# A two-layer kernel on one core: other buffers for sorted tokens, another reciprocal root in the layer norm, and a second sequence that ends in two halves

## The chip, the core and the metric

The kernel runs on one core of a Trainium2 chip. The core has five engines that run side by side and wait for each other through semaphores: TensorE (PE in the profile) for matrix products, VectorE (DVE), ScalarE (ACT), GpSimd (POOL), and SyncE (SP), which here only issues transfers. The metric is the device time of one execution in microseconds (us); lower is better.

## The reference

Two transformer layers work on x of shape 2 x 1024 x 128 (two sequences of 1024 tokens), all in float32.

```python
x  = L0_attn_x
xn = layernorm(x)                                   # no gain, no bias
x  = x + attn0(xn) + ffn0(xn)
xn = layernorm(x)
x  = x + attn1(xn) + ffn1(xn)
```

- attn0: 16 heads of 8; queries, keys and values are xn times signs; a causal mask; the weight is sigmoid(4 * score / sqrt(8)), without a softmax.
- ffn0: softmax gate over 32 experts, 4 chosen per token, each an MLP 128 -> 64 -> 128 (silu(x w1 + b1) * (x w3 + b3), then w2), and a shared expert of width 128.
- attn1: projections, 16 heads, a relative position term with radius 128, softmax over all 1024 keys, output projection.
- ffn1: sigmoid gate over 16 experts, 4 chosen, each of width 176, and a shared expert of width 352.

## The kernel before

TensorE's order is written out by hand; the other engines' instructions are placed by a scheduler that follows their dependences. Within each engine instructions run in order, so an instruction that waits holds up all that stand behind it.

Layer 0's attention is a list of 96 steps (`steps0`: sequence, group of 4 heads, half of the queries, tile of 128 keys), the *cycles*. In cycle c TensorE computes scores (`scores0(c)`, L724), ScalarE takes the sigmoid (L730), GpSimd masks the diagonal tiles (L736), and one cycle later TensorE multiplies with the values (`values0(c-1)`, L751). A first half of queries has 4 cycles and a second half 8, of which the last 4 are on the diagonal and narrower. Cycles 48 to 95 are the second sequence's. All else in layer 0 is hung on this list: `at(c, f, ..., slot)` puts f before the scores of cycle c (slot 0), between scores and values (`MID`), or after the values (`END`).

Sequence 0's experts are computed densely: 34 *units*, each a pair of experts or the shared expert for 512 tokens. `open_unit` makes both first products (L359, L360) in one `big` tile of PSUM, then the activation, the product, and the weighting; `close_unit` (L387) makes the second product two cycles later in the `ffn` bank.

Sequence 1's tokens are sorted by expert. `scatter0` writes each normalized token to a slot in DRAM (GpSimd, indirect), and sixteen *quads* of four blocks of 128 slots are then computed, one every 1.5 cycles from cycle `QUADS`: `fetch0` (SP loads tokens and four weight blocks, cycle c-3), `turn0` (TensorE transposes the tokens, L639, and VectorE copies them out, L641; cycle c-1), `hidden0` (L651, with L657, L659 and L660 as activation), `outputs0` (L668; the next quad's cycle). From DONE + 2, `gather0` (L680) fetches each token's rows again and `gathered0` (L689) adds them, two per cycle. What a loaded weight set is good for ends with its outputs, so `fetch0` reuses the space of w1, w3 and w2 in turn.

PSUM has eight banks: three `big` tiles of two banks each, one `acc` bank for values, and one `ffn` bank that closing units, turns and hidden products share. `small()` is half of a `big` tile.

After the attention of sequence b, `added0` adds attention and shared expert (GpSimd), `merged0` transposes the sum into the residual x2s (L769, L770), `normed1` takes layer 1's norm, `turned1` transposes it (L253), and `blocks1` lists the six units of layer 1's shared expert. For the second sequence this follows cycle 96, together with the first ten `scan` steps of layer 1's attention (row maxima, L1173 on TensorE, L1193 and L1198 on VectorE), whose operands (`operands`, L1105) live in a pool that opens when layer 0's pool is closed. Then layer 1's main loop begins (first L1224), with 128 steps.

`layernorm` computes the reciprocal root with ScalarE's Sqrt (L235) and five short VectorE instructions (L237 to L241). Sqrt and Sigmoid are in different function tables, so ScalarE loads a table at each change. `turned_biases` (L514) transposes b1 and b3 and is the first thing that TensorE does; `biased0` (cycle 33) uses the result.

Of the kernel before, what the change touches and what calls it, by code (L numbers as in the profile page):

```python
# [10 lines left out]
F32 = mybir.dt.float32  # L11
AF = mybir.ActivationFunctionType
# [5 lines left out]
P = 128  # L18
# [30 lines left out]
def fused_layers_kernel(ctx: ExitStack, tc: tile.TileContext, a: dict, out: bass.AP):  # L49
# [39 lines left out]
    def quads(t):  # L89
        return t.rearrange("p (i c) -> p i c", c=P)  # L90
# [24 lines left out]
    w1 = load(l0, "w1", [P, E0 * I0])  # L115
    w3 = load(l0, "w3", [P, E0 * I0])
    b1 = load(l0, "b1", [P, M0])
    b3 = load(l0, "b3", [P, M0])
    w2 = load(l0, "w2", [P, M0, D], a["w2"].rearrange("(m p) d -> p m d", p=P))
# [103 lines left out]
    def layernorm(x, xn, pool, tiles=range(NT)):  # L223
# [6 lines left out]
        root = pool.tile([P, NT], F32, tag="ln_root", name="ln_root")  # L230
# [4 lines left out]
        nc.scalar.activation(root[:, c], var[:, c], AF.Sqrt)  # L235

        nc.vector.reciprocal(t[:, c], root[:, c])  # L237
        nc.vector.tensor_mul(t[:, c], t[:, c], var[:, c])
        nc.vector.tensor_add(t[:, c], t[:, c], root[:, c])
        nc.vector.tensor_scalar(t[:, c], t[:, c], 0.5, None, ALU.mult)  # L240
        nc.vector.reciprocal(rstd[:, c], t[:, c])  # L241
# [109 lines left out]
    def open_unit(weigh=nc.gpsimd):  # L351
# [12 lines left out]
        if ba is None:  # L364
            e = nc.scalar.activation(sg[0:m], hh[0:m, 0, :], AF.Sigmoid)
            last_exp["name"] = e.ins.name
            nc.scalar.copy(t[0:m], hh[0:m, 1, :])
            nc.vector.tensor_mul(sg[0:m], hh[0:m, 0, :], sg[0:m])
            nc.gpsimd.tensor_mul(h[0:m], t[0:m], sg[0:m])
# [138 lines left out]

    def turned_biases():
# [6 lines left out]
        return t  # L516
# [74 lines left out]
    def biased0(b):  # L591

        ps = small()
        for m in range(2):
            for h in range(2):
                for i in range(2):
                    nc.tensor.matmul(
                        ps[I0 * h:I0 * (h + 1), m * NBLK0 // 2:(m + 1) * NBLK0 // 2], b13[:, m, I0 * i:I0 * (i + 1)],
# [21 lines left out]
    def fetch0(g):  # L620
        w = l0.tile([P, 4, 2 * P], F32, tag=("w1", "w3", "w2")[g % 3], name="bw0")
# [4 lines left out]
        x = moe.tile([P, 4, P], F32, tag="t", name="bx0")  # L626
# [8 lines left out]
    def turn0(g):  # L635
        ps = quads(psum["ffn"].tile([P, TB], F32, tag="ffn", name="turn"))
# [6 lines left out]
    def hidden0(g):  # L643
# [9 lines left out]
        t = moe.tile([P, 4, P], F32, tag="h", name="bh0", bufs=4)  # L653
        sg, quad_h[g] = t[:, 0:2, :], t[:, 2:4, :]
# [36 lines left out]
    def blocks0(b):  # L691
        parts = [
            (P, w1[:, m * P:(m + 1) * P], w3[:, m * P:(m + 1) * P], w2[:, m, :], b1[:, m:m + 1],
# [66 lines left out]
    def added0(b):  # L760
        for q in range(NB):
            nc.gpsimd.tensor_add(yT0[b, q], yT0[b, q], attn0[b][:, q * TB:(q + 1) * TB])

    def merged0(b):
        x2s[b] = const.tile([P, NT, D], F32, tag=f"x2{b}", name=f"x2{b}")
        for q in range(NB):
# [10 lines left out]
    def turned1(b):  # L777
        xT1[b] = const.tile([P, T], F32, tag=f"xT1{b}", name=f"xT1{b}")
        transpose_tokens(xn1[b], xT1[b])
# [807 lines left out]
```

## Time and profile before

| | us |
|---|---|
| median of 3 runs (1307.63 to 1309.75) | 1308.75 |
| the profiled execution's own time | 1320.37 |
| its span, first to last instruction | 1318.5 |
| TensorE busy | 1171.2 (89%) |
| VectorE busy | 770.8 (58%) |
| ScalarE busy | 626.0 (47%) |
| GpSimd busy | 378.6 (29%) |
| mean granted TensorE clock | 0.945 |

An engine's busy time is the time covered by its instructions. In a list of waits, a line names the waiting instruction, what released it, the sum of the waits in us, their number and the longest. In a timeline, a line has the start and the time in us, engine, source line, operation, tile written and tile read, shapes and the number of instructions, and in brackets the idle time before and its releaser; "issue" means that no releaser was found. In a table of stages each engine has its busy time and its number of instructions; PEclk is the clock that TensorE was granted, as a share of full speed.

### The profile page before, as it was taken

To read this page: it belongs to the slowest core of one execution; us is meant where nothing else is said; L and a number is where in the kernel's file an instruction comes from. 1 tells how busy PE (TensorE), PEld (TensorE's weight loads), DVE (VectorE), ACT (ScalarE), POOL (GpSimd) and SP (SyncE) were. 2 spreads that over 40 slices of the span, in tenths; PEclk is the share of its full clock that TensorE was granted. 3 is DMA by queue.
4 is the path that set the end of the run, shared out by engine and by line. 5 is a ranking of instruction groups with operands and counts; after the bars stand their busy time and mean duration, and the time that the engine had idled before them with its cause. 6 is when DMAs were issued, how large, how long until landed. Compare 5 with 4: busy or idle time off the path is not lost.

```text
span 1318.5 us, 23960 instructions
## 1 busy us (share of the span) xinstructions
PE 1171.2 (89%) x8781; PEld 576.3 (44%) x8781; DVE 770.8 (58%) x2335; ACT 626.0 (47%) x1123; POOL 378.6 (29%) x482
## 2 busy tenths in 40 slices
PE   4889899887988778899799999998999999998997
PEld 1233233344432233434344444447999444443433
DVE  5564754446423377676876756754555766766563
ACT  2653344554555322464355644543444555554553
POOL 1124144410135342001002443330000345445463
PEclk9899999997998769899899998988999999998998
DMA  6955842334614250344265644658998255663510
GB/s 185 249 143 155 241 125 80 92 110 127 180 42 127 64 192 21 124 143 145 97 193 175 202 147 148 218 169 264 285 291 249 89 185 165 207 204 122 166 60 28
DMA packets 194472, 204.76 MB, mean 155 GB/s; under 512 B 26388, under 2 KB 176148, under 8 KB 194100
## 3 DMA queue, kind: packets, MB, share of 16 engines
q1 hardware_dynamic: 188052, 190.12, 46.9%
q0 software_dynamic: 6304, 13.12, 3.3%
q8 instruction: 69, 1.13, 0.4%
q14 instruction: 47, 0.39, 0.1%
HBM read 121.29 MB, written 90.42 MB: 161 GB/s over the span
## 4 chain that ended last, share of the span: by engine, by line
PE 67%; DVE 15%; DMA 5%; issue 5%; ACT 5%; POOL 2%; SPq 0%; DVEq 0%; POOLq 0%; ACTq 0%
PE sm L1234 11%; PE sm L1173 9%; PE acc L1253 8%; PE sm L1224 6%; PE big L724 5%; PE acc L751 4%; PE sm L975 4%; PE big L359 3%; DVE junk L1193 3%; PE big L360 3%; DVE maxima L1198 2%; PE ffn L387 2%; PE sm L1124 2%; DMA blockw<-wx 2%; PE sm L990 2%
## 5 line engine op out<-in xcount | busy, mean ns | idle before, releaser
L1241 ACT ACTIVATE p<-sm 128x512 f32<-128x512 f32 x512 | 264.7, 607 | 235.0 <-PE sm L1234 234.5
L1198 DVE TENSOR_REDUCE maxima<-sm 128x1 f32<-128x512 f32 (+3 forms) x472 | 226.8, 502 | 100.2 <-PE sm L1173 100.2
L730 ACT ACTIVATE at<-big 128x1024 f32<-128x1024 f32 (+1 forms) x192 | 145.1, 809 | 149.8 <-PE big L724 145.6
L1193 DVE CUSTOM_DVE_ANT_0 junk<-sm,near 128x384 f32<-128x384 f32 (+2 forms) x292 | 130.3, 446 | 69.7 <-PE sm L1173 69.7
L1253 PE MATMUL acc<-p,vs 128*32 128x512 f32 (+1 forms) x1288 | 147.2, 526 | 0.4 <-ACT yu L1265 0.4
L1224 PE MATMUL sm<-ident,near 128*128 128x128 f32 x704 | 109.3, 289 | 24.6 <-DVE maxima L1198 11.4
L1234 PE MATMUL sm<-qa,kls 32*128 32x512 f32 (+3 forms) x832 | 114.7, 569 | 0.0
L724 PE MATMUL big<-qm,xT 32*128 32x512 f32 (+3 forms) x768 | 108.1, 577 | 6.9 <-DVE h L373 4.0
L1173 PE MATMUL sm<-kls,qs 32*128 32x512 f32 (+2 forms) x776 | 108.0, 584 | 6.3 <-POOL kls L1105 5.3
L1224 PEld LDWEIGHTS sm<-ident,near 128*128 128x128 f32 x704 | 78.7, 144 | 79.2 <-ACT p L1241 35.4
L901 POOL DMA_INDIRECT got<-slots_y,slot_of x64 | 64.7, 1011 | 168.7 <-ACT p L1241 157.5
L751 PE MATMUL acc<-at,xn 128*32 128x512 f32 (+3 forms) x768 | 89.3, 540 | 21.4 <-POOL at L736 15.1
L736 POOL TENSOR_SCALAR_AFFINE_SELECT at<-at 128x512 f32<-128x512 f32 x64 | 41.9, 656 | 185.0 <-ACT at L730 184.6
L889 POOL DMA_INDIRECT slots_x<-xn,slot_of x64 | 62.4, 974 | 97.7 <-ACT p L1241 88.0
L1128 ACT COPY rel<-sm 128x512 f32<-128x512 f32 x112 | 57.5, 600 | 64.4 <-PE sm L1124 64.4
L911 POOL TENSOR_SCALAR got<-got,share 128x128 f32<-128x128 f32 x64 | 41.8, 654 | 109.3 <-DMA got<-slots_y,slot_of 109.0
L1173 PEld LDWEIGHTS sm<-kls,qs 32*128 32x128 f32 x776 | 37.1, 189 | 82.4 <-ACT p L1241 21.0
L1253 PEld LDWEIGHTS acc<-p,vs 128*32 128x32 f32 x1288 | 26.6, 109 | 106.2 <-issue 95.7
L1124 PE MATMUL sm<-posd,qs 32*128 32x256 f32 x448 | 57.4, 422 | 12.4 <-DVE maxima L1198 11.4
L724 PEld LDWEIGHTS big<-qm,xT 32*128 32x128 f32 x768 | 38.8, 198 | 67.0 <-issue 41.5
L1105 POOL TENSOR_SCALAR khs<-kf,not_aux,k_add 128x1024 f32<-128x1024 f32 x8 | 9.6, 1200 | 177.4 <-PE sm L1234 177.4
L1234 PE MATMUL sm<-qa,khs 32*128 32x512 f32 (+3 forms) x512 | 60.4, 507 | 0.0
(334 smaller groups left out, 1754.8 us busy)
## 6 DMA issues: line engine op xcount, KB each, us to landing
bounce<-rel SPq DMA_DIRECT2D x64, 768.0 KB
near<-bounce SPq DMA_DIRECT2D x64, 768.0 KB
blockw<-wx SPq DMA_DIRECT2D x53, 304.0 KB
slots_y<-by SPq DMA_DIRECT2D x35, 256.0 KB
cb<-cw SPq DMA_DIRECT2D x64, 128.0 KB
bw<-wx SPq DMA_DIRECT2D x64, 128.0 KB
room<-wx SPq DMA_DIRECT2D x26, 304.0 KB
slots_x<-zeros SPq DMA_DIRECT2D x19, 256.0 KB
```

What stands on the lines that cost most here:

```text
L724: nc.tensor.matmul(halves[r // 2][:, r % 2, off:TB], xT0[b][g, kt * P:(kt + 1) * P], masked[b, s][g, q * TB + off:(q + 1) * TB], start=Tru ...
L730: e = nc.scalar.activation(at[:, 2 * j:2 * j + 2, off:TB], sc[:, :, off:TB], AF.Sigmoid, scale=4.0 / math.sqrt(HD))
L751: nc.tensor.matmul(y[32 * r:32 * r + 32, off:TB], xn0[b][:, kt * P + 32 * r:kt * P + 32 * r + 32], at[:, r, off:TB], start=(kt == 0), stop ...
L901: d = nc.gpsimd.indirect_dma_start(y, None, slots_y[:, :], bass.IndirectOffsetOnAxis(ap=slot_of[:, t, j:j + 1], axis=0))
L1124: nc.tensor.matmul(ps[r][:, j, :], qs[g, t:t + P], posd[g, :], start=True, stop=True)
L1173: nc.tensor.matmul(ps[r][:, (k0 - lo) * P:(k1 - lo) * P], qs[g, qt * P:(qt + 1) * P], (kh if far else kl)[g, k0 * P:k1 * P], start=True, s ...
L1193: nc.vector.tensor_tensor_reduce(junk[:, 0:(k1 - k0) * P], part, near[n, i][:, r, w0:w0 + (k1 - k0) * P], 1.0, -BIG, ALU.add, ALU.max, mx[ ...
L1198: nc.vector.tensor_reduce(mx[:, r, slot:slot + 1], part, AX.X, ALU.max)
L1224: nc.tensor.matmul(ps[r][:, i * P:(i + 1) * P], near[n, i][:, r, w0:w0 + P], ident, is_transpose=True, start=(i == close[0]), stop=False, ...
L1234: nc.tensor.matmul(ps[r][:, i0 * P:i1 * P], k[g, kt * P:(kt + 1) * P], qa[n][g, i0 * P:i1 * P], start=(m == 0 and not close), stop=(m == l ...
L1241: e = nc.scalar.activation(p[:, r, :], ps[r], AF.Exp)
L1253: nc.tensor.matmul(y[rows_of(r), part], vs[:, kt, rows_of(r)], probs[n, kt][:, r, part], start=(kt == 0), stop=(kt == NT - 1 and part.stop ...
```

## The change

It has these parts, all but the norm within layer 0 and the passage to layer 1:

1. `turned_biases` moves from before cycle 0 to cycle 32, and `biased0` to 34.
2. w1, w3 and w2 are loaded in halves of their own. `fetch0` runs at c-5 and takes these six buffers in turn; tokens take four buffers. `turn0` transposes into a half of a `big` tile instead of the `ffn` bank. In `hidden0` the sigmoid and the product are two tiles. `QUADS` goes from 54 to 57.
3. The 34 units are spread over 38 cycles. `added0`, `merged0`, `normed1`, `turned1` and the gate of sequence 0 move by 3 to 6 cycles; projections of layer 1 move from two cycles after DONE to four before it.
4. Gathers start one cycle after DONE, their additions one cycle behind them. Eight units stand on the cycles after DONE (before, five, with three more at the end); their last product is on VectorE, without ScalarE's copy.
5. `added0`, `merged0`, `normed1`, `turned1` and `blocks1` of sequence 1 are split: the first 512 tokens at cycles 90 to 95, the rest after cycle 96.
6. The reciprocal root is made on VectorE: a first guess from the bits, and three Newton rounds.

```diff
-        root = pool.tile([P, NT], F32, tag="ln_root", name="ln_root")
-        nc.scalar.activation(root[:, c], var[:, c], AF.Sqrt)
-        nc.vector.reciprocal(t[:, c], root[:, c])
...
-        nc.vector.reciprocal(rstd[:, c], t[:, c])
+        bits = t.bitcast(I32)[:, c]
+        nc.vector.tensor_scalar(bits, var.bitcast(I32)[:, c], 1, None, ALU.arith_shift_right)
+        nc.vector.tensor_scalar(rstd.bitcast(I32)[:, c], bits, -1.0, float(0x5F3759DF), ALU.mult, ALU.add)
+        for _ in range(3):
+            nc.vector.tensor_mul(t[:, c], rstd[:, c], rstd[:, c])
+            nc.vector.tensor_mul(t[:, c], t[:, c], var[:, c])
+            nc.vector.tensor_scalar(t[:, c], t[:, c], -0.5, 1.5, ALU.mult, ALU.add)
+            nc.vector.tensor_mul(rstd[:, c], rstd[:, c], t[:, c])
...
-            nc.scalar.copy(t[0:m], hh[0:m, 1, :])
+            if weigh is nc.gpsimd:
+                nc.scalar.copy(t[0:m], hh[0:m, 1, :])
             nc.vector.tensor_mul(sg[0:m], hh[0:m, 0, :], sg[0:m])
-            nc.gpsimd.tensor_mul(h[0:m], t[0:m], sg[0:m])
+            weigh.tensor_mul(h[0:m], t[0:m] if weigh is nc.gpsimd else hh[0:m, 1, :], sg[0:m])
...
-        w = l0.tile([P, 4, 2 * P], F32, tag=("w1", "w3", "w2")[g % 3], name="bw0")
+        w = l0.tile([P, 4, 2 * P], F32, tag=("w10", "w11", "w30", "w31", "w20", "w21")[g % 6], name="bw0")
...
-        x = moe.tile([P, 4, P], F32, tag="t", name="bx0")
+        pool, tag = ((moe, "t"), (moe, "t"), (l0, "xn0"), (l0, "xT0"))[g % 4]
+        x = pool.tile([P, 4, P], F32, tag=tag, name="bx0")
...
-        ps = quads(psum["ffn"].tile([P, TB], F32, tag="ffn", name="turn"))
+        ps = quads(small())
...
-        t = moe.tile([P, 4, P], F32, tag="h", name="bh0", bufs=4)
-        sg, quad_h[g] = t[:, 0:2, :], t[:, 2:4, :]
+        sg, quad_h[g] = (moe.tile([P, 2, P], F32, tag="h", name=n, bufs=4) for n in ("bsg0", "bh0"))
...
-    b13 = turned_biases()
...
+    QUADS = 57
+    SPAN = QUADS - 6 - U0
     for i in range(HALF):
-        at(U0 + i, open_unit, nc.gpsimd if U0 + i < 30 else nc.vector, slot=MID)
-        at(U0 + 2 + i, close_unit, slot=END)
+        c = U0 + i * SPAN // HALF
+        at(c, open_unit, nc.gpsimd if c < 30 else nc.vector, slot=MID)
+        at(c + 2, close_unit, slot=END)
...
+    at(32, turned_biases, slot=MID)
+    at(34, biased0, 1, slot=MID)
...
-    QUADS = 54
-        at(c - 3, fetch0, g, slot=END)
+        at(c - 5, fetch0, g, slot=END)
...
-        at(DONE + 2 + i // 2, gather0, 1, i, slot=END)
-        at(DONE + 4 + i // 2, gathered0, 1, i, slot=END)
+        at(DONE + 1 + i // 2, gather0, 1, i, slot=END)
+        at(DONE + 2 + i // 2, gathered0, 1, i, slot=END)
...
-    at(DONE + 2, projections, 0, slot=MID)
-    at(DONE + 2, queries, 0, 0, slot=END)
+    for i in range(8):
+        c = DONE + 1 + 2 * i
+        at(c, open_unit, nc.vector, slot=MID)
+        at(c + 2, close_unit, slot=END)
+    at(DONE - 4, projections, 0, slot=MID)
+    at(DONE - 2, queries, 0, 0, slot=END)
...
-    for i in range(5):
-        at(DONE + 4 + 3 * i, open_unit, slot=MID)
-        at(DONE + 6 + 3 * i, close_unit, slot=END)
...
-    at(N_ATT + 1, added0, 1)
-    at(N_ATT + 2, merged0, 1)
+    at(90, added0, 1, (0,))
+    at(91, merged0, 1, (0,), slot=END)
+    at(92, normed1, 1, FIRST)
+    at(94, turned1, 1, (0,), slot=END)
+    at(95, blocks1, 1, (0,))
+    at(N_ATT + 1, added0, 1, (1,))
+    at(N_ATT + 2, merged0, 1, (1,))
+    at(N_ATT + 2, normed1, 1, LAST)
...
     at(N_ATT + 3, operands, 0, 0)
+    at(N_ATT + 3, cleared1)
...
-    at(N_ATT + 3, normed1, 1)
+    at(N_ATT + 4, turned1, 1, (1,), slot=MID)
+    at(N_ATT + 5, blocks1, 1, (1,))
...
-    at(SCAN + 2, turned1, 1, slot=MID)
-    at(SCAN + 3, blocks1, 1)
-    for i in range(6):
-        at(SCAN + 3 + i, open_unit, slot=MID)
-        at(SCAN + 5 + i, close_unit, slot=END)
+    for i in range(3):
+        at(SCAN + 1 + 2 * i, open_unit, nc.gpsimd, slot=MID)
+        at(SCAN + 3 + 2 * i, close_unit, slot=END)
```

## The prediction

> **What bounds the kernel now.** I read four views: busy time by stage, the list of TensorE's waits, the timeline around the longest waits, and the chain that ended last. From 524.6 us on, where layer 1's main loop begins, the change alters neither the work nor its order, so that stretch (793.9 us to the end of the 1318.5 us span) is taken as constant and all terms lie before it. The stages below are: cycles 48 to 53 of layer 0, the sixteen quads (cycles 54 to 77), the tail of layer 0 (78 to 95), and the passage to layer 1.
>
> ```profile
> core 0: us, PE busy (x) PEld busy (x) DVE busy (x) ACT busy (x) POOL busy (x), PEclk, DMA share, GB/s
> 238.95:260.82 21.87, 16.12 (x121) 6.63 (x120) 9.00 (x34) 12.52 (x16) 9.60 (x12) 0.95 0.22 67
> 260.82:372.92 112.10, 94.92 (x805) 49.44 (x804) 53.39 (x156) 59.28 (x102) 10.38 (x16) 0.92 0.46 131
> 372.92:460.24 87.32, 71.36 (x398) 24.76 (x394) 25.88 (x52) 41.03 (x64) 43.60 (x48) 0.84 0.26 80
> 460.24:524.62 64.38, 51.80 (x215) 22.57 (x211) 50.19 (x150) 16.33 (x29) 21.88 (x34) 0.84 0.28 98
> ```
>
> TensorE is the busiest engine in every stage, but idles 5.8 + 17.2 + 16.0 + 12.6 = 51.5 us, and its granted clock is below 1: (1 - clock) x busy gives 0.8 + 7.6 + 11.4 + 8.3 = 28 us. So about 80 us of these 286 us are waits and their aftermath; that is all the change can win here. In the last stage VectorE is nearly as busy, and becomes the floor. What TensorE waits for:
>
> ```profile
> PE big L514 <- DMA b<-in_b_dram: 16.2, 1, 16.2
> PE acc L751 <- POOL at L736: 15.1, 9, 4.4
> PE turn L639 <- issue: 11.4, 6, 3.6
> ...
> PE acc L751 <- ACT at L730: 6.4, 3, 2.9
> ...
> PE turn L639 <- PE big L668: 2.5, 3, 0.8
> ```
>
> No entry names the loads of tokens (bx) or of expert weights (bw). Three of these waits in the timeline:
>
> ```profile
> 16.24 0.37 PE L514 MATMUL big<-ident,b 128*16 128x128 f32 x1 [16.24 <-DMA b<-in_b_dram]
> ...
> 19.68 4.85 PE L724 MATMUL big<-qm,xT 32*128 32x512 f32 x16 [2.00 <-DVE qm L717]
> ```
> ```profile
> 267.82 0.35 DVE L660 SCALAR_TENSOR_TENSOR bh<-hidden,bias,bh 128x128 f32<-128x128 f32 x1
> 268.27 0.63 PE L639 MATMUL turn<-ident,bx 128*128 128x128 f32 x4 [3.60 <-issue]
> 268.83 1.90 PE L724 MATMUL big<-qm,xT 32*128 32x512 f32 x8
> ```
> ```profile
> 391.99 0.96 POOL L680 DMA_INDIRECT got<-slots_y,slot  x1 [0.30 <-issue]
> 392.96 0.64 POOL L736 TENSOR_SCALAR_AFFINE_SELECT at<-at 128x512 f32<-128x512 f32 x1
> ...
> 393.66 1.08 PE L751 MATMUL acc<-at,xn 128*32 128x256 f32 x8 [4.43 <-POOL at L736]
> ...
> 394.67 2.08 PE L387 MATMUL ffn<-h,sdw 128*128 128x512 f32 x2
> ```
>
> First: TensorE's first instruction transposes a bias that lands at 16.2 us, with the token transposes queued behind it. Second: the "issue" wait is the one ffn bank; the turn starts 0.1 us after L660, the bank's last reader, ends (268.17). Third: the causal mask stands behind gathers on POOL.
>
> **The change part by part** (minus is a gain).
>
> *Start.* turned_biases goes from before cycle 0 to cycle 32. The first four normalized tiles then set the start. bv_q's arrival (7.35 us) still stands in VectorE's order, now after two of the three rounds; 14 small instructions took 1.25 us there, so the 16 left take about 1.5 us (8.8), normalizing 4 tiles and the masks between them about 2 us (10.9), transposes to 11.4, the copy 0.7 and qm 0.5 with what stands between: first scores near 13.5 instead of 19.7. **-6** (ends -3, -6.6). The two transposes and copy reappear at cycle 32, under 1.2 us, beside attention work.
>
> *Loads.* w1, w3, w2 in halves: three more SP issues of 0.43 to 0.9 us early, moving later constants by 2 us; the first expert unit runs at 99.6 us. 0. Fetching at c-5 instead of c-3, six weight and four token buffers: SP's wait for an old quad's weights (41.3 us at L632) goes, but TensorE never waited for these loads. 0; if the cover went (quads faster than the four 128 KB loads), it would show as hidden waiting for bw.
>
> *Units of sequence 0* spread over 38 cycles instead of 34. From 160 to 240 us TensorE is busy 79 of 80 us; the work, about 7 us of it, moves to cycles 48 to 51 and is paid there. 0 (-2 to +2), as some of it fills the 3.0 us of mask waits there.
>
> *Quads.* turn0 takes a big bank, so TensorE does the next scores (1.1 us) before it needs the ffn bank for hidden0. sg and h as two tiles let the second sigmoid start without waiting for the first product (0.8 us, as at 267.03). Of the nine turn waits (13.9 us) I leave 1.7 us, from the longest: 3.6 - 1.1 - 0.8. Late next: hidden's copy bxT (3.0 us in two waits, kept; layer 1's gate still stands before it on VectorE), and a new coupling: scores, turn and outputs now rotate over three big banks, ten allocations per three cycles instead of eight. I allow 16 x 0.2 = 3 us. Idle 17.2 -> 9.
>
> *Layer norm without Sqrt.* Seven table loads of 1.28 us go from ScalarE's list. Where cycles are short (254 to 264 us, four of them) one wait of 2.7 us goes. VectorE gets 14 short instructions instead of 5 per call, each about 0.2 us with its dependence: +1.8 us per call, hidden in the quads (VectorE 53 of 112 us). Not hidden is the call for the last half-sequence: turned1 stands before the scans in TensorE's order, with only some 5.4 us of matmuls between merge and turn. Here a rule speaks against the change. The row: VectorE's ln_t steps at 469.6, 470.2 and 471.4 took 0.56, 1.20 and 0.98 us beside POOL's 1.2 us operand instructions, 0.16 us elsewhere. The Trainium skill, "SBUF — State Buffer", section "Who interferes with whom", says that a VectorE instruction with two SBUF inputs is blocked for the whole of a GpSimd instruction that reads SBUF. By the rule all nine products of the call could each lose a POOL instruction, +9 us; by the changed order POOL has only four long ones there (kls, khs, vs, h: 4.7 us) and the eight statistics, with one input, run beside them first. I take +3.
>
> *Tail.* It is shorter by three cycles and holds eight units instead of six opened. Their last product goes from POOL (1.27 us each) to VectorE (0.69), and ScalarE's copy (0.58) goes. POOL then has 32 gathers at 1.25 us pitch, 11 masks of 0.64, two additions of 1.27: 49.6 us, against about 54 us of TensorE work (scores and values 24, units 25, the rest 5, from their rows). gathered0 stands one cycle after its gather instead of two; landing takes 2.5 us, and VectorE already waits 50.1 us for gathers here. Behind those waits stand the two products that free a unit's big bank. Projections move ahead of DONE past the last quads, without new work; by_position's bounce writes stay behind the quads' fetches on SP. I leave 9 of 16.0 us idle.
>
> *Passage.* Half of the second sequence's merge, norm and transpose and two units (6 us of TensorE) move into layer 0. VectorE: 50.2 us now; minus half the norm 5.5, two sigmoid products 1.4, half a merge and a copy 1.4; plus the steps 2.6 and one product 0.7: 45.2 us, 33 of them the ten scans' maxima. The operands come before the 16 memsets (2.4 us on POOL). With VectorE as floor and the wait for the norm ahead of the scans, about 52 us instead of 64.4: **-12** (-3 to -17).
>
> *Clock.* The row: after the 4.43 us wait L387 took 2.08 us where it takes 1.12 elsewhere, and L360 follows at 1.02; after the 2.50 us wait at 408.4 it again took 2.08. The Trainium skill, "TensorE: Matmul & The Clock Gate", Part 1, says that the clock halves after an idle window of about 3.4 us. By the rule only the four or five longest waits cost extra, some 1.7 us each (half a window, an estimate from the page), 8 us in all; by the rows 28 us run slow. I take the rows: shorter waits also matter. Half of the slow time of cycles 48 to 95 (19.8 us) stays.
>
> *Sum for cycles 48 to 96.* TensorE's work at full clock: 182.4 - 19.8 = 162.6 us; plus 7 (moved from earlier, saved there) and 7 (two units, half a merge and half a transpose from the passage): 176.6. Plus idle 3 + 9 + 9 and slow 10 = 207.6, against 221.3: -13.7, with the 7 saved earlier -21. Counting the matmuls of each changed cycle by their full-clock rows instead gives 172.5 + 24 = 196.5, hence -32. I take the first, since its stages are measured: **-21** (-8 to -34).
>
> Total -6 - 21 - 12 = **-39 us** on the profiled execution (1320.4 us, span 1318.5). The median of the runs, 1308.75 us, is 0.9% below it; scaled, -38.7: about 1270 us.
>
> **The rivals.**
> *The waits move.* hidden0 waits where turn0 did, masks wait behind gathers as before, and only the start (-6), the tables (-3) and some of the passage (-6) come: 1294 us. For it: one ffn bank remains, POOL is 49.6 us full, VectorE waits for gathers. Against: 1.1 us of scores between. 19%.
> *Slower: scores wait for ScalarE in the bank rotation.* With a turn between, scores take a bank that the previous cycle's sigmoid has to have read. The second sigmoid ends 2.1 us after its scores end (275.68, 277.79); TensorE has about 3.2 us (hidden, values, outputs) in between. Beyond 1.1 us more delay each cycle pays; over 24 cycles the gain of 38 us is gone at 1.6 us a cycle. At the 2.7 us of the one wait for L730, it costs 65: 1308.75 + 27 = 1336 us. ScalarE is busy 59 of 112 us. 7%.
> *The change does more than its waits*: the count by matmuls holds and the passage reaches VectorE's floor: -6 - 32 - 17 = -55, 1254 us. 17%.
>
> **Numbers.** Forecast case 57%, 1270 us (1258 to 1284). Slower by over 0.2% (2.6 us, about what a measurement of this kernel can tell from no change): 8%, the bank case and 1% of the case where the waits move; within it: 2%, of the latter too; faster: 90%. The range reaches to both gaining rivals: 1252 to 1296.
>
> **What would show it.** First L724 near 13.5 us; no Sqrt table load; turn with no wait for bh's readers; quads at 4.2 instead of 4.7 us a cycle; attention's last values near 433 us; main loop from about 486 us. Wrong would be: big banks waiting for L730 every cycle, hidden waiting for bw, or a passage over 60 us.

## The result, and the profile after

The changed kernel takes 1292.43 us (median of 4 runs, 1290.72 to 1295.13); beside it the kernel before took 1308.19 us (4 runs). The ratio is 0.9887, 95% interval [0.9855, 0.992]. Measured again later, in a set of its own, it was 1289.47 us against 1309.98, ratio 0.9839 [0.9795, 0.9883]. So the change saves 16 to 21 us. The forecast was 39 us (1270 us); the measured time lies inside the range, near its slow end. The ratios leave out executions more than 1.5% above the fastest of their kernel as slow, which among all kernels here strikes only two of the six of e_sqrt (its ratio would be 0.983 with them).

The profiled execution took 1295.13 us (span 1293.0, mean clock 0.956). First its table of stages, with columns as before. The quads start three cycles later now, so the rows are cycles 48 to 56, the quads (57 to 80), the tail of layer 0 (81 to 95), and the passage to layer 1.

```profile
core 0: us, PE busy (x) PEld busy (x) DVE busy (x) ACT busy (x) POOL busy (x), PEclk, DMA share, GB/s
226.14:253.84 27.70, 26.18 (x171) 8.47 (x171) 8.57 (x12) 15.47 (x20) 8.71 (x10) 1.00 0.48 145
253.84:361.79 107.95, 100.34 (x828) 55.68 (x825) 59.86 (x205) 60.51 (x104) 10.64 (x16) 0.95 0.40 116
361.79:436.29 74.50, 62.99 (x360) 22.02 (x359) 33.72 (x84) 33.25 (x53) 36.78 (x43) 0.93 0.30 92
436.29:505.79 69.50, 47.03 (x192) 20.03 (x191) 49.56 (x147) 10.35 (x19) 19.73 (x33) 0.78 0.28 95
```

Layer 0 as a whole behaves as forecast: TensorE idles 1.5 + 7.6 + 11.5 = 20.6 us in the first three rows (39 before), the clock there is 0.93 to 1.00, and attention ends at 436.3 us instead of 460.3. The last row is the surprise. In the passage TensorE is *less* busy than before (47 us against 52), with six units in it instead of eight. And yet the passage is 5 us *longer*, with 22.5 us idle and a clock of 0.78.

The list of TensorE's waits in the quads has lost its nine turn waits (13.9 us); this is what stands there now (who waits, for whom: us in all, times, longest):

```profile
PE hidden L659 <- DVE bh L667: 3.9, 2, 3.6
PE hidden L659 <- DVE bxT L649: 2.2, 3, 1.6
```

And the list for the passage, whose first entry was not there before:

```profile
PE big L256 <- DVE xn L246: 8.7, 1, 8.7
PE big L1184 <- DVE maxima L1204: 2.9, 3, 1.4
PE big L1219 <- DVE negmax L1212: 2.2, 1, 2.2
PE big L777 <- POOL yT L769: 2.0, 1, 2.0
```

L256 is the transpose of the last half-sequence (`turned1`, L253 before). It stands ahead of the scans in TensorE's order and waits for the last normalized tile. The timeline just before shows what that tile was late for:

```profile
451.46 1.26 POOL L373 TENSOR_TENSOR h<-t,sg 96x512 f32<-96x512 f32 x1 [0.67 <-DVE ln_t L242]
451.49 1.28 DVE L243 TENSOR_SCALAR ln_t<-ln_t 128x4 f32<-128x4 f32 x1
452.71 1.20 POOL L1116 TENSOR_SCALAR kls<-kf,not_aux,k_add 128x1024 f32<-128x1024 f32 x1
452.80 0.19 DVE L244 TENSOR_TENSOR ln_rstd<-ln_rstd,ln_t 128x4 f32<-128x4 f32 x1
453.03 0.90 DVE L241 TENSOR_TENSOR ln_t<-ln_rstd 128x4 f32<-128x4 f32 x1
453.89 1.19 POOL L1116 TENSOR_SCALAR khs<-kf,not_aux,k_add 128x1024 f32<-128x1024 f32 x1
453.96 1.13 DVE L242 TENSOR_TENSOR ln_t<-ln_t,ln_var 128x4 f32<-128x4 f32 x1
455.03 1.03 POOL L1119 COPY vs<-vf 128x1024 f32<-128x1024 f32 x1
455.12 0.96 DVE L243 TENSOR_SCALAR ln_t<-ln_t 128x4 f32<-128x4 f32 x1
456.12 0.16 DVE L244 TENSOR_TENSOR ln_rstd<-ln_rstd,ln_t 128x4 f32<-128x4 f32 x1
...
456.32 1.11 DVE L246 TENSOR_SCALAR xn<-x,ln_mv,ln_rstd 128x128 f32<-128x128 f32 x4
...
456.81 1.15 PE L256 MATMUL big<-ident,xn 128*128 128x128 f32 x4 [8.68 <-DVE xn L246]
```

Read the two engines against each other. Each VectorE step has 4 elements per partition and needs 0.16 us when it is alone. Four of them take about 1 us here, and each begins within 0.35 us after a GpSimd instruction of 1.0 to 1.3 us has begun and ends just after it. I call such a step *held*. Not every step beside GpSimd is: L244 at 452.80 also begins just after kls and takes 0.19 us, and these rows don't show why. kls, khs and vs in these rows are the *second* set of operands, `operands(0, 1)`, which the program lists six cycles after the first; GpSimd's order has it right behind the memsets and a unit's product. From the merge of the half-sequence (442.13) to its last tile (457.43) the norm takes 15.3 us.

### The profile page after: what moved, and what is told of

The parts are those of the page before. It is cut to its first block, busy times and chain, and to the rows that moved or that the text cites. A ratio compares the mean times of both kernels' runs of the same rounds, so it can differ in the third digit from the quotient of the medians.

```text
span 1293.0 us, 24010 instructions
## 1 busy us (share of the span) xinstructions
PE 1161.0 (90%) x8781; PEld 577.1 (45%) x8781; DVE 782.9 (61%) x2420; ACT 613.0 (47%) x1102; POOL 370.4 (29%) x475
## 4 chain that ended last, share of the span: by engine, by line
PE 63%; DVE 19%; DMA 8%; issue 5%; ACT 3%; POOL 2%; SPq 0%; POOLq 0%; DVEq 0%; ACTq 0%
PE sm L1245 11%; PE sm L1184 8%; PE acc L1264 8%; PE sm L1235 5%; PE big L731 4%; PE acc L758 4%; PE sm L984 4%; DVE maxima L1209 3%; PE big L362 3%; DVE junk L1204 3%; PE sm L1135 3%; PE big L363 2%; DMA got<-slots_y,slot_of 2%; PE ffn L391 2%; DMA room<-wx 2%
## 5 line engine op out<-in xcount | busy, mean ns | idle before, releaser
L1204 DVE CUSTOM_DVE_ANT_0 junk<-sm,near 128x384 f32<-128x384 f32 (+2 forms) x292 | 130.3, 446 | 64.3 <-PE sm L1184 63.9
L1184 PE MATMUL sm<-kls,qs 32*128 32x512 f32 (+2 forms) x776 | 105.8, 572 | 6.7 <-POOL kls L1116 5.4
L1184 PEld LDWEIGHTS sm<-kls,qs 32*128 32x128 f32 x776 | 36.5, 186 | 80.8 <-ACT p L1252 21.1
L1135 PE MATMUL sm<-posd,qs 32*128 32x256 f32 x448 | 58.1, 422 | 11.9 <-DVE maxima L1209 10.9
L1245 PE MATMUL sm<-qa,khs 32*128 32x512 f32 (+3 forms) x512 | 60.9, 509 | 0.0
```

The costliest lines, as they stand in the source:

```text
L1135: nc.tensor.matmul(ps[r][:, j, :], qs[g, t:t + P], posd[g, :], start=True, stop=True)
L1184: nc.tensor.matmul(ps[r][:, (k0 - lo) * P:(k1 - lo) * P], qs[g, qt * P:(qt + 1) * P], (kh if far else kl)[g, k0 * P:k1 * P], start=True, s ...
L1204: nc.vector.tensor_tensor_reduce(junk[:, 0:(k1 - k0) * P], part, near[n, i][:, r, w0:w0 + (k1 - k0) * P], 1.0, -BIG, ALU.add, ALU.max, mx[ ...
L1245: nc.tensor.matmul(ps[r][:, i0 * P:i1 * P], k[g, kt * P:(kt + 1) * P], qa[n][g, i0 * P:i1 * P], start=(m == 0 and not close), stop=(m == l ...
```

## Experiments

Three questions were open: whether layer 0's parts are worth what the sum said; why the passage grew; and whether it is bounded by VectorE's work. Theory A: TensorE waits in the passage because the transpose stands ahead of the scans. Theory C: the norm is long because GpSimd's instructions hold its small steps. Rival B: VectorE's work is a floor, so that neither matters. The times in the table are from one profile of each kernel; "first scan" and "passage" count from attention's last values, and the passage ends where the main loop starts.

| kernel | ratio to before | attention ends | first scan | passage | main loop from |
|---|---|---|---|---|---|
| before | 1 | 460.3 | +13.1 | 64.3 | 524.6 |
| before, again (r_before) | 1 | 460.7 | +13.1 | 64.3 | 525.0 |
| changed | 0.9887 [0.9855, 0.992] | 436.3 | +25.0 | 69.5 | 505.8 |
| changed, again (r_after) | 0.9839 [0.9795, 0.9883] | 431.0 | +24.5 | 68.7 | 499.7 |
| bias transposes first (u_bias) | 0.9912 [0.9882, 0.9942] | 437.7 | +25.3 | 68.6 | 506.3 |
| turns in the ffn bank (u_bank) | 0.9901 [0.9864, 0.9939] | 438.6 | +26.1 | 71.8 | 510.4 |
| Sqrt on ScalarE (e_sqrt) | 0.9796 [0.9743, 0.985] | 436.3 | +21.2 | 64.7 | 501.0 |
| late turn (e_turn_late) | 0.9827 [0.9784, 0.987] | 438.9 | +18.0 | 64.5 | 503.4 |
| second operands after the norm (e_pool) | 0.9823 [0.9774, 0.9873] | 433.3 | +23.6 | 68.1 | 501.4 |
| quiet GpSimd (e_quiet) | 0.979 [0.9747, 0.9834] | 432.9 | +19.6 | 65.1 | 498.0 |
| quiet, late turn (e_quiet_late) | 0.977 [0.9726, 0.9814] | 438.9 | +14.8 | 60.3 | 499.2 |
| the same with Sqrt (e_quiet_late_sqrt) | 0.9813 [0.9779, 0.9848] | 432.7 | +15.2 | 61.8 | 494.5 |
| units behind the scans (e_units_after) | one run | 428.8 | +26.1 | 79.1 | 507.9 |
| part 5 undone (u_split) | 0.9749 [0.9707, 0.9791] | 427.3 | +7.8 | 60.9 | 488.2 |
| the same, second operands late (u_split_quiet) | 0.9726 [0.9678, 0.9774] | 429.6 | +7.7 | 60.9 | 490.5 |
| units' product on GpSimd (u_late_start) | 0.9892 [0.9838, 0.9946] | 434.3 | +26.2 | 70.9 | 505.3 |

Two yardsticks come first.

**The kernel before, again.**

> The kernel before once more, for a second profile. The first profiled execution took 1320 us, 11.6 us over its median; the changed kernel's two profiles were within 3 us of theirs. If the first profile of before was simply a slow execution, this one is nearer to 1310 us, and attention ends a few us before 460 and the main loop takes less than 794 us; the passage (64.3 us) should stay within 2 us, since its waits are of a fixed length. If the main loop takes 794 us again, then the change does alter it (782 to 789 us in all kernels with the change).

It took 1312.61 us (span 1310.9), with attention's end and the passage the same within 0.4 us. Its main loop took 1310.9 - 525.0 = 785.9 us instead of 793.9. So the 8 us by which the first profile was longer lay in the main loop alone, which the change doesn't touch (782 to 794 us in all these kernels).

**The changed kernel, again.**

> The changed kernel itself, for comparison with the three others on the same chip. It was 0.9887 of the kernel before; on the chip of the first experiments, where that kernel takes some 1312 us, this would be 1297 us. Its passage was 69.5 us; two variants with the same passage code (bias transposes first; turns in the ffn bank) had 68.6 and 71.8 us, with TensorE waiting 11.3 us for the norm instead of 8.7, so I expect 68.5 to 72 us here. No theory separates on this run.

The passage is the same (68.7 us, of which 8.2 us is the wait for xn), but attention ends at 431.0 instead of 436.3 us. The code is the same; the last three half-passes of attention, from about 345 us on, took 87.7 us here and 90.9 us there, and up to 92.8 us in the other kernels that share this code. A difference of less than 5 us in attention's end, seen in one profile each, therefore says nothing. In both profiles TensorE waits 8 to 9 us for xn. In u_bias, u_bank and u_late_start below, whose passage has the same code, it waits 11.3 us: there one more step, the shift L238, was held for 3.60 us, and merge to last tile takes 16.2 us instead of 14.9 to 15.3.

**Undo the start (part 1).**

```diff
-    at(32, turned_biases, slot=MID)
+    turned_biases()     # before cycle 0
```

> The changed kernel with the bias transposes back ahead of cycle 0, nothing else undone. If the start is worth what the two profiles show (first scores at 12.6 us instead of 19.7), the run is 6 to 7 us slower than the changed kernel (1298 to 1300 us) and the profile shows the first instruction waiting for b1 and b3 until about 16 us. If later waits absorb the start (cycles paced by loads or by the gate), it is less than 3 us slower.

The first scores come at 19.85 us instead of 12.61: the 7.2 us are there. But after the third half-pass of attention only 2.8 us were left, at cycle 48 4.3 us (6.0 against the second profile), and the ratio is higher than the changed kernel's by 0.0025 to 0.0073, 3 to 10 us, within intervals that overlap. The start's gain is real; how much of it reaches the end was not resolved.

**Undo the banks of the turn (part 2).**

```diff
-        ps = quads(small())
+        ps = quads(psum["ffn"].tile([P, TB], F32, tag="ffn", name="turn"))
```

> The changed kernel with turn0 back in the one ffn bank, all else as changed (loads ahead, two tiles for sigmoid and product). If the bank was the cause of the turn waits (13.9 us before), the quads get 6 to 12 us longer than the changed kernel's 108 us, and turns wait again for bh's readers. If the separate tiles had already removed the waits, or the bank rotation gives it back, it is within 2 us.

In this kernel's list of TensorE's waits the old entry is back:

```profile
PE turn L647 <- issue: 10.8, 6, 4.4
```

From the last values of cycle 51 to those of cycle 75 it takes 108.2 us instead of 102.3, so the banks are worth 5.9 us there. At attention's end 2.3 us are left, which is within the spread just named. In no kernel with the change do scores wait for the sigmoid each cycle: the forecast's slower rival did not occur.

**Undo the move of the units' product (part 4).** This is the kernel labelled u_late_start, a name that does not describe it.

```diff
-        at(c, open_unit, nc.vector, slot=MID)
+        at(c, open_unit, nc.gpsimd, slot=MID)
```

> The changed kernel, with the last product of the eight units on the last cycles of layer 0 back on GpSimd (and ScalarE's copy with it), as before the change. I counted GpSimd as 49.6 us full in that stretch and the move to VectorE as part of the gain there. If GpSimd's gathers set the pace of the tail, eight products of 1.27 us delay the gathers by up to 10 us, and attention ends 3 to 10 us later, with masks waiting behind gathers again; ratio higher than the changed kernel's by 0.002 to 0.007. If TensorE's own work and its clock set it, as the spread of the tail between executions of the same code suggests (87.7 to 92.4 us), attention ends within 3 us of the changed kernel's 431 to 439 us and the ratio is the same within its interval.

The last gather is issued at 437.0 us and attention ends at 434.3 us. Both lie between the two profiles of the changed kernel (433.3 and 438.8 us, 431.0 and 436.3 us), and the ratio lies in its interval. GpSimd doesn't pace the tail by more than the spread.

**The turn later (theory A).**

```diff
-    at(N_ATT + 4, turned1, 1, (1,), slot=MID)
-    at(N_ATT + 5, blocks1, 1, (1,))
+    at(N_ATT + 7, turned1, 1, (1,), slot=MID)
+    at(N_ATT + 8, blocks1, 1, (1,))
...
-        at(SCAN + 1 + 2 * i, open_unit, nc.gpsimd, slot=MID)
-        at(SCAN + 3 + 2 * i, close_unit, slot=END)
+        at(SCAN + 3 + 2 * i, open_unit, nc.gpsimd, slot=MID)
+        at(SCAN + 5 + 2 * i, close_unit, slot=END)
```

> The changed kernel with the second half's transpose (turned1 of sequence 1, blocks 1) three cycles later, behind the first scans, and its three units two cycles later. Theory A, the passage lost the gain because TensorE stands before that transpose waiting for the norm (8.7 us) while the scans queue behind it: the scans start some 5 to 8 us earlier and the run is 5 to 8 us faster than the changed kernel (about 1286 us). Theory B, VectorE is the floor of the passage in any order: the wait moves to the maxima and the time stays within 2 us of the changed kernel's.

The wait for xn is gone and the passage falls to 64.5 us. But the first scan still starts 18.0 us after attention, 5 us later than in the kernel before. In the list of waits of its passage a closing unit has taken the place:

```profile
PE ffn L391 <- POOL h L373: 3.3, 1, 3.3
```

That h is a product on GpSimd, which waits for a product of VectorE (L372) that stands between the norm's held steps. So A is true and not the whole.

**Sqrt back (part 6 alone undone).** `layernorm` as before the change, all else as changed.

> The changed kernel with the layer norm of before: Sqrt on ScalarE and five short VectorE steps instead of fourteen. If the fourteen steps on VectorE are what makes the last norm long, the passage gets 3 to 5 us shorter, and the tables cost 2 to 4 us among the quads: within 2 us of the changed kernel in all. If the tables are the larger part, it is 3 to 6 us slower.

The passage is 64.7 us, and merge to last tile takes 11.5 us: six short instructions, one of them on ScalarE, offer GpSimd less to hold than the fourteen of Newton's rounds. ScalarE has 23 table loads of 1.28 us in its order here against 10 with Newton, and yet layer 0 ends at 436.3 us, as in the first profile of the changed kernel. The ratio is lower by 0.004 to 0.009 (0.001 to 0.006 with all executions). So no gain from the tables that part 6 avoids is seen, though one of a few us would be lost in the spread of attention's end.

**GpSimd out of the way (theory C), in two steps.** First, the second set of operands waits for the last normalized tile (`last_norm`, recorded in `layernorm`):

```diff
-            nc.gpsimd.tensor_scalar(t, kf, ...)
+            e = nc.gpsimd.tensor_scalar(t, kf, ...)
+            if (b, s) == (0, 1):
+                tc.add_manual_dep(e.ins, last_norm["name"], ...)
...
-        nc.gpsimd.tensor_copy(vs, v)
+        e = nc.gpsimd.tensor_copy(vs, v)     # the same dependence
```

> The second set of operands (kls, khs, vs of sequence 0, second group) has to wait on GpSimd until the last normalized tile is written; nothing else changes. Theory C (GpSimd's operand instructions hold the norm's small VectorE steps): the steps that took 0.90, 1.13 and 0.96 us beside these three instructions fall to about 0.17 us, so merge to last normalized tile takes about 12.8 us instead of 15.3, and TensorE's wait for xn shrinks by the same 2.5 us; ratio lower than that of the changed kernel by 0.002. Theory B (VectorE's work is the floor): VectorE has as much to do, so the passage stays within 1 us. Theory A (only the place of the turn in TensorE's order costs) says nothing of the length of the norm: it stays 15.3 us.

The three steps take 0.16, 0.16 and 0.17 us now. But in this execution another step was held: L240 (the shift, L238 in the changed kernel) took 3.60 us, from 443.61 to 447.21, beside a unit's product and then the memsets:

```profile
443.53 1.25 POOL L376 TENSOR_TENSOR h<-t,sg 128x512 f32<-128x512 f32 x1
443.61 3.60 DVE L240 TENSOR_SCALAR ln_t<-ln_var 128x4 int32<-128x4 int32 x1
444.73 0.14 POOL L1131 MEMSET vs<- 128x32 f32 x1
444.79 2.39 POOL L1068 MEMSET negmax<- 128x128 f32 x16
```

So against the changed kernel's own profiles little is gained: merge to last tile is 13.7 us instead of 14.9 to 15.3, and the wait for xn is 8.7 us. The fair comparison is with u_bias, u_bank and u_late_start, where the shift was held for the same 3.60 us. Against these merge to last tile falls from 16.2 to 13.7 us and the wait from 11.3 to 8.7, by the 2.5 us that theory C gives the three steps. Second, the memsets wait too, and the two units that open after attention make their product on VectorE:

```diff
-                nc.gpsimd.memset(t, 0.0)
+                e = nc.gpsimd.memset(t, 0.0)     # after last_norm, too
...
-    at(N_ATT + 2, open_unit, nc.gpsimd, slot=MID)
+    at(N_ATT + 2, open_unit, nc.vector, slot=MID)
...
-    at(N_ATT + 3, open_unit, nc.gpsimd)
+    at(N_ATT + 3, open_unit, nc.vector)
```

> As the run before, and also the 16 memsets of negmax wait for the last normalized tile, and the two expert units that open after attention make their last product on VectorE instead of GpSimd. Between merge and norm GpSimd then runs only the first kls, khs and vs. Theory C: the steps that took 1.60 and 1.28 us beside the units' products are short too; merge to last normalized tile near 10 us, TensorE's wait near 3.5 us, the passage 4 to 6 us shorter than that of the changed kernel, ratio lower by 0.003 to 0.005. Theory B: VectorE gets 1.4 us more work, so the passage stays or grows by 1 us. Theory A: as B.

Every step but one is short now (the first took 0.95 us, beside the first vs). The end of the norm in this kernel's timeline:

```profile
447.08 0.17 DVE L245 TENSOR_SCALAR ln_t<-ln_t 128x4 f32<-128x4 f32 x1
447.29 0.16 DVE L246 TENSOR_TENSOR ln_rstd<-ln_rstd,ln_t 128x4 f32<-128x4 f32 x1
447.49 1.11 DVE L248 TENSOR_SCALAR xn<-x,ln_mv,ln_rstd 128x128 f32<-128x128 f32 x4
448.66 2.40 POOL L1068 MEMSET negmax<- 128x128 f32 x16 [5.28 <-DVE xn L248]
```

Merge to last tile: 438.93 to 448.60, 9.7 us. TensorE's wait is 4.64 us, the passage 65.1 us. So C is shown: the norm is over 5 us shorter when GpSimd is quiet, although VectorE has two products more to do, and the passage is 3.6 to 4.4 us shorter. Not all of it is held steps. These give back 4.2 us; the rest is order, above all the wait for ScalarE's copy of a unit, which this kernel doesn't make (2.3 us before, now a wait of 0.2 us for the sigmoid).

**Both.**

> The quiet GpSimd of the run before, and the transpose of the last half-sequence two scans later, as in the experiment with the late turn (64.5 us, ratio 0.983). If A and C are both true and lie one behind the other: in the late version the first scan still started only 18 us after attention, because TensorE closed a unit whose product stood behind the norm's held steps on VectorE; a short norm frees that too. I expect the first scan 13 to 14 us after attention, a passage of 60 to 61 us and a ratio of 0.979 to 0.981. If A alone is true: 64 to 65 us, as with the late turn. If B is true, VectorE's 50 us set a floor of about 55 us that none of these reaches.

First scan at +14.8 us, passage 60.3 us: the two gains add, as they do if the waits lie one behind the other on one chain.

**Both, with Sqrt.**

> Quiet GpSimd and late turn, with the norm's root on ScalarE again. With Newton this kernel was 0.977, its passage 60.3 us. If Newton's steps cost only because GpSimd held them, the two roots are now equal: passage 59 to 61 us, ratio 0.975 to 0.979. If the table loads themselves cost something in the short cycles, as I assumed (3 us), this one is slower: ratio 0.978 to 0.981. If the fourteen steps cost TensorE time even in quiet, it is faster: 0.973 to 0.975.

Passage 61.8 us, ratio 0.9813 against 0.977, with intervals that overlap. With GpSimd quiet, Sqrt has lost its advantage in the passage: Newton's steps cost because they were held. Whether the tables cost a few us elsewhere stays open; the intervals don't tell.

**Part 5 undone.** Merge, norm and transpose of the second sequence stand whole after attention again, the transpose behind the third scan, all six units between the scans.

```diff
-    at(90, added0, 1, (0,))
...
-    at(N_ATT + 3, open_unit, nc.gpsimd)
-    at(N_ATT + 4, close_unit, slot=END)
-    at(N_ATT + 4, turned1, 1, (1,), slot=MID)
...
+    at(N_ATT + 1, added0, 1)
+    at(N_ATT + 2, merged0, 1, range(NB))
...
+    at(N_ATT + 3, normed1, 1)
...
+    at(SCAN + 2, turned1, 1, slot=MID)
+    at(SCAN + 3, blocks1, 1)
+    for i in range(6):
+        at(SCAN + 3 + i, open_unit, slot=MID)
+        at(SCAN + 5 + i, close_unit, slot=END)
```

> Part 5 undone, all other parts kept: the second sequence is merged and normalized whole after attention, its transpose stands behind the third scan as before, all six units of layer 1's shared expert stand between the scans. Theory A and C (TensorE waits for a norm that GpSimd stretches): with the turn behind the scans nothing waits for the norm, so the first scan starts 11 to 14 us after attention instead of 25, the scans take 51 us instead of 44.5, the passage 62 to 65 us instead of 69; attention ends 1 to 3 us earlier; the ratio is lower than the changed kernel's by 0.003 to 0.006. Had part 5 gained as I predicted, the undone kernel would be slower by 12 us (0.009).

The first scan starts 7.8 us after attention and the passage is 60.9 us: 8 to 9 us shorter than with part 5, although the same six units lie in it (six instead of three of them between the scans) and half a merge and half a transpose more. The work that part 5 had moved is missing from layer 0: its last three half-passes take 80.7 us, and 87.4 to 92.8 us in all kernels that keep part 5. The ratio is 0.9749, below both measurements of the changed kernel with no overlap of the intervals. What I had counted as the largest gain of the passage was a loss of 0.009 to 0.014 of the whole time. This kernel is faster than both.

**Part 5 undone, second operands late.**

> Part 5 undone as in the last experiments (0.9749, passage 60.9 us), and the second set of operands and the 16 memsets on GpSimd wait for the last normalized tile. With part 5 undone TensorE did not wait for the transpose, but once for maxima (8.2 us) whose VectorE instructions stood behind the norm, and three of the norm's steps took 3.35, 0.96 and 2.13 us beside memsets and operands instead of 0.17 each, 5.9 us in all. If GpSimd's instructions hold these steps wherever the transpose stands, this wait falls to 2 to 4 us and the passage to 55 to 57 us, near the 52 us that I predicted; ratio 0.971 to 0.973. If the held steps cost only because a transpose waited for them, the passage stays at 60 to 61 us and the ratio at 0.975. A new wait would be for the second operands themselves, which the fifth scan needs some 25 us after the norm, so I expect none.

The memsets did not move: in this order the program lists them ahead of the norm, so that they waited for an earlier one, and the step beside them still took 3.35 us. The steps beside the operands went from 0.96 and 2.13 us to 0.17 each. The wait that stood behind the norm shrank as theory C says, by 2.7 us; this is its line in the list of part 5 undone, and then in this kernel's:

```profile
PE big L1135 <- DVE maxima L1209: 8.2, 1, 8.2
```
```profile
PE big L1147 <- DVE maxima L1221: 5.5, 1, 5.5
```

And the passage did not shrink, neither to my 55 to 57 us nor at all. From the first scan to the main loop the windows of the two kernels are these, without and with the late operands:

```profile
435.05:488.15 53.10, 41.34 (x185) 17.80 (x185) 46.55 (x140) 10.23 (x19) 15.62 (x29) 0.83 0.34 119
```
```profile
437.23:490.51 53.28, 43.86 (x184) 18.89 (x185) 44.53 (x140) 10.24 (x19) 16.05 (x29) 0.79 0.34 118
```

VectorE is 2.0 us less busy, and TensorE 2.5 us busier with the same matmuls at a clock of 0.79 instead of 0.83. So the shorter wait and the slower matmuls offset each other in these two profiles. That the one caused the other is not shown.

**What bounds the scans (rival B).** The three units go behind the last scan:

```diff
-        at(SCAN + 1 + 2 * i, open_unit, nc.gpsimd, slot=MID)
-        at(SCAN + 3 + 2 * i, close_unit, slot=END)
+        at(SCAN + 10 + i, open_unit, nc.gpsimd, slot=MID)
+        at(SCAN + 11 + i, close_unit, slot=END)
```

> The three units between the scans stand behind the last scan instead. It tells what bounds the scans, which took 44.5 us where I had counted VectorE's 33 us. If VectorE's maxima are the floor, first scan to the last maxima stays about 40 us, since 3 us of the units' products are all that leaves VectorE. If scans and units alternate (the two big tiles of a scan and the one of a unit have to be read by VectorE before the next can begin), each unit costs its TensorE time of about 3 us, and the stretch falls by 7 to 9 us, to 36 us; what is gained there is paid again behind the scans, so the main loop starts within 2 us of where it did.

First scan to last maxima, the changed kernel (second profile) and this one:

```profile
455.46:499.72 44.26, 32.41 (x160) 13.60 (x159) 33.07 (x109) 6.43 (x12) 3.78 (x3) 0.85 0.11 37
```
```profile
454.87:493.47 38.60, 31.79 (x140) 15.37 (x140) 30.58 (x105) 2.64 (x5) 0.00 (x0) 0.54 0.12 41
```

The stretch falls by 5.7 us, 2.5 of which are VectorE's, and the result lies between my two numbers. VectorE's work is not a floor that is reached: it idles 11 us with the units between the scans and 8 us without. How far the units are covered this run can't tell, because the clock (the third number from the end) differs: it is 0.54 without them instead of 0.85, and the same 112 matmuls of the scans (L1184) take 32.3 us instead of 19.3. Behind the scans, with little beside them, the units take 14 us, so the main loop begins later (507.9 us).

## Why the prediction was wrong

**The passage: -12 us, measured +5.1 and +4.4. This is the step that failed**, and 16 to 17 us of the shortfall. It read: "With VectorE as floor and the wait for the norm ahead of the scans, about 52 us instead of 64.4". The prediction's own sign of being wrong, a passage over 60 us, came. Three terms of the sum were wrong.

1. *The norm.* I took +3 us for steps held beside GpSimd, because by the changed order GpSimd had "only four long ones there (kls, khs, vs, h)". There were eight: the second set of operands and a second unit's product ran in the same stretch. Five steps were held, 1.60, 1.28, 0.90, 1.13 and 0.96 us instead of 0.16 to 0.18, which is 5.0 us; e_quiet gives 4.2 of them back. This could be seen before. Three of the five (L235, and L243 twice) have one tensor as input, and the rule as I read it spoke of two; but one of the three rows that I set against the rule was already such a step, held beside the copy of vs:

```profile
471.29 1.03 POOL L1108 COPY vs<-vf 128x1024 f32<-128x1024 f32 x1
471.39 0.98 DVE L240 TENSOR_SCALAR ln_t<-ln_t 128x8 f32<-128x8 f32 x1
```

   The rest of the 15.3 us is order: two products of a unit (L372, 0.7 us each) and a wait of 2.3 us for ScalarE's copy stood in VectorE's order between the norm's steps.
2. *What stands ahead.* I saw that the transpose stands before the scans with 5.4 us of matmuls between merge and turn, and put no price on the rest of the wait. The first scan moved from +13.1 to +25.0 us. Moving the turn gives 7 us of these 12 back, a quiet GpSimd 5; part 5 undone starts at +7.8.
3. *The floor.* VectorE was busy 49.6 us (45.2 forecast; the difference is about the held steps) but idle 20 of 69.5 us. A busy share gives the length of a stage only if nothing else puts the engines in turn. From the first scan to the main loop VectorE has 33 us of work, the units' products included, and the stretch takes 44.5. TensorE waits there for VectorE's maxima and negmax (in the list of the passage above), and VectorE waits for the units. Its product L372 of a unit follows the unit's matmuls on TensorE and a sigmoid and a copy on ScalarE, and the maxima behind it in VectorE's order wait with it. This is over half of VectorE's 11 us of idle time; for scores it waits 0.4 us. From its list of waits in that stretch:

```profile
DVE sg L372 <- ACT t L371: 5.9, 2, 3.6
```

The order that I called safe, fewer units between the scans, did bring its share: that stretch fell from 51.2 to 44.5 us. It was paid for ahead of it: +11.9 - 6.7 = +5.2 us.

**The start, -6: right in size** (12.61 us instead of 19.68, -7.1), with an open question on how much reaches the end.

**Cycles and units, -21: right.** Start and cycles together were -27 at attention's end; the two profiles of the changed kernel give -24.0 and -29.7. Idle time in cycles 48 to 95 was forecast as 3 + 9 + 9 us and is 1.5 + 7.6 + 11.5. The turn waits went (u_bank brings them back), and the mask waits of the tail fell to 0.2 us. Some of the turns' wait came back as forecast by the first rival, in small: hidden0 waits 3.9 us for the readers of the ffn bank, where I had left 1.7, and 2.2 us for bxT, where I had left 3.0. One sign did not come: quads at 4.2 us a cycle instead of 4.7. The row of before ends where the scores of cycle 79 start, so it spans 25 cycles and a cycle took 4.5 us; now 24 cycles take 107.95 us, again 4.5.

**Clock: the row was the better guide.** Slow time of cycles 48 to 95, (1 - clock) x busy, was forecast as 10 us by halving what the rows show; it is 0 + 5.0 + 4.4 = 9.4. Only one wait there is over 3.4 us (3.6), which by the rule would have left some 1.7 us. The half was a guess, so that it fits this well is in part luck. In the passage the clock of 0.78 was not foreseen: after the 8.68 us wait the next four matmuls of L391 took 3.62 us, where a pair takes 1.02 elsewhere.

**Loads at nothing: consistent.** No wait of TensorE for tokens or the quads' weights appeared. It was not tried alone.

**Layer norm's tables, one wait of 2.7 us: no gain was seen**, and one of this size could not have been (e_sqrt).

**The baseline.** By profiles before and after the change took 25.5 and 26.7 us, by medians 16 and 20.5. The main loop, which has the same instructions, takes 782 to 794 us in single executions, so a sum of this size against one profile is uncertain by several us. With the passage's 17 us put right, the forecast would have been -22. The time measured is that of the first rival (1294 us), but not by its way: most of layer 0's waits went, and the passage, which gains 6 us there, lost.

## What to carry to other kernels

A stage is not as short as its busiest engine's work: look at the order in which each engine alternates with the next, and price every wait ahead of the first instruction of the long part. Before moving a chain of tiny dependent instructions onto VectorE, list what GpSimd runs beside it *in its compiled order*, hoisted work included, and let that work wait for the chain's end. Splitting a stage so that half of it overlaps earlier work is a loss if the other half then stands ahead of the work that used to hide it.

## What the hardware showed

- A VectorE step with a single SBUF tensor as input was held as well as one with two: L243 (128x4) took 1.28 us and L235 took 1.60 us beside GpSimd's products, 0.16 to 0.18 us elsewhere. The Trainium skill, "SBUF — State Buffer", section "Who interferes with whom", lists `tensor_scalar` too among what can contend with GpSimd, when it runs in a mode that uses both of VectorE's ports. Both steps are of that kind; which mode they ran in no run here shows.
- Memsets, which read nothing, can hold a step. The shift was held until the 16 memsets had ended in u_bias, u_bank, u_late_start and e_pool (3.60 us each) and, with part 5 undone, in u_split and u_split_quiet (3.35 us each); in e_units_after L235 was (3.66 us). Yet in both profiles of the changed kernel L235, which began beside the same product ahead of the memsets, came free after 1.25 to 1.60 us, and the next steps ran in 0.16 to 0.28 us beside the same memsets. What decides between the two is not known; where the step is held to the end, TensorE's wait for xn is 10.1 to 11.3 us instead of 8.2 and 8.7.
- A shorter wait did not bring a shorter slow stretch. In u_split, after 8.2 us of waiting, matmuls took up to twice their usual time for some 7 us (446.6 to 453.6); in u_split_quiet, after 5.5 us, for some 13 us (446.0 to 459.4).
- No long wait is needed for a low clock: in e_units_after it was 0.54 for 38.6 us, with no wait of TensorE over 2.2 us.
